# A second weight combination with shared products, copied by ScalarE into the accumulator's bank

## The chip, the cores and the metric

The kernel runs on one core of a Trainium2 chip. The metric is device time in microseconds (us). Engines are named as in the profile: PE is TensorE (PEld its weight loads), DVE VectorE, ACT ScalarE, POOL GpSimd, SP SyncE.

## The reference

A residual block of four modulated 1-D convolutions over x of 128 samples x 64 channels x 1024 positions, in float32. Each sample has its own weights: the layer's shared weights, scaled by the sample's style and normalised.

```python
def _layer(x, style, w, b, mw, mb, typ):
    s = style @ mw.T + mb
    weight = SCALE * w * s[:, None, :, None]
    demod = lax.rsqrt(jnp.sum(weight * weight, axis=(2, 3)) + EPS)
    weight = weight * demod[:, :, None, None]
    if typ == 'same':
        out = vmap(conv_same)(x, weight) + b
    elif typ == 'upsample':
        out = blur(vmap(conv_up)(x, weight) + b, 2.0 * blur_k, (1, 1))
    elif typ == 'downsample':
        out = vmap(conv_down)(blur(x, blur_k, (2, 2)), weight) + b
    return out

out = x
for i, typ in enumerate(('same', 'upsample', 'same', 'downsample')):
    out = _layer(out, style, weights[i], biases[i], mod_w[i], mod_b[i], typ)
return x + out
```

## The kernel before, in words

Since no layer has a nonlinearity, the kernel folds the four convolutions of a sample into one filter of nine taps of 64 x 64 weights, and then convolves x with it. The samples go in 32 **quads** of four. Four samples fill the array: each product is four matmuls of 64 x 64, one for each quarter of the array (the loops over rows and cols in HALF), and in the profile each matmul is two MATMUL records with a weight load each.

For a quad the filter is made in four steps. **scale3** (ACT) scales layer 3's weights into two wd tiles. **stage1** combines them with layer 2's weights in PSUM (psS), and ACT and DVE scale the result into an S tile. From iteration 0 on it is split: stage1_a has three products, after which ACT copies blocks 0 to 3 of S; stage1_b has two products, after which DVE makes blocks 4 and 5 (two scalar_tensor_tensor), and POOL adds block 0 onto block 2. A block is 64 columns. **stage2** (R) convolves S with the table E, which holds the nine taps of layer 1 with the blur in it; it has nine products, of three blocks where the tap's number is even and of two where it is odd, 23 blocks in all, into psR; ACT scales psR into two R tiles. **stage3** (W) combines R with layer 0's weights in two parts, and ACT scales them into Wf, from which DVE makes the tiles H (combine_a, combine_b).

The convolution itself takes five products of three taps each (conv0 to conv4, all through product()), 340 columns wide, on x as it is (T04, T3) or combined by DVE and POOL (in_g01, in_g2, in1, in2, in3, in04). conv0 to conv3 accumulate in psA of the quad, conv4 in Y; DVE combines them (sum1, sum2), and ACT makes the outputs (output), which SP stores.

The order on every engine is written out by hand in the loop over q. Iteration q finishes quad q, while it convolves n = q + 1, makes the filter of c = q + 2 (stage2, stage3), and S of s = q + 3. For most q, PE's order is: stage2(c), conv4(q), stage3(c, 0), conv3(n), stage3(c, 1), conv0(q, 0), conv1(n, 0), stage1_a(s), conv1(n, 1, 2), conv0(q, 1), stage1_b(s), conv0(q, 2), conv2(n). ACT's order at the end of an iteration is: S of stage1_a, output(q, 1), output(q, 0), scale3(s + 1), then R of the next iteration. DVE's is: sum1(n), the two S instructions, and then sum2 at the start of the next iteration.

The iterations in SLOTS (1 to 3, 5 to 7, 9, 12, 14, 19, 25) have other products in the place of stage1_a; stage1_a then stands in the place of stage1_b, and stage1_b behind conv2's first tap. EXTRA hangs small work on certain places.

PSUM has eight banks, and psS, psR, psW and psE all take turns in one pair of them (the pool ps_w has one buffer for each of the tags u0 and u1). psA has two buffers of two banks each, of which 340 of 512 columns are used; Y has the last pair. A matmul with start=True marks the whole bank as empty; one with start=False adds where a matmul has written since, and overwrites elsewhere.

Of the kernel before, what the change touches and what calls it, by code (L numbers as in the profile page):

```python
# [48 lines left out]
F32 = mybir.dt.float32  # L49
AF = mybir.ActivationFunctionType  # L50
ALU = mybir.AluOpType
# [3 lines left out]
C = 64  # L55
# [8 lines left out]
def kernel(  # L64
# [293 lines left out]
    def scaled_copy(eng, dst, src, f):  # L358
        if eng is nc_a:
            nc_a.activation(dst, src, AF.Copy, scale=f)  # L360
        else:
            eng.tensor_scalar(dst, src, f, None, op0=ALU.mult)
# [33 lines left out]
                )  # L396

    def s_tiles(q):
        t = s_pool.tile([P, 2, 6, C], F32, tag="S", name=f"S{q}")
        return [t[:, r] for r in range(2)], t  # L400

    def flat(t):
        return t.rearrange("c a o -> c (a o)")
# [3 lines left out]
    def stage1(q, pool=None, engs=(nc_a, nc_a), between=None):  # L407

        wd = chain[q]
        ps = unit(pool or ps_w, f"psS{q}")  # L410
        for k, (at, at1) in enumerate(((0, 3), (3, 1), (1, 4))):
            tap_matmul(ps, wd, at, 2, woi[2][:, k, :], EVEN, first=k == 0)
            tap_matmul(ps, wd, at1, 1, woi[2][:, k, :], slice(1, 2), last=k == K - 1)
        if between:
            between()
        st, _ = s_tiles(q)
        for r in range(2):
            scaled_copy(engs[r], flat(st[r][:, 1:]), ps[r][:, : 5 * C], tB[:, q, r : r + 1])
        chain[q] = st
        return ps  # L420

    def stage1_a(q):

        ps = unit(ps_w, f"psS{q}")
        wd = chain[q]
        tap_matmul(ps, wd, 1, 2, w2n[:, 0, :], EVEN, first=True)
        tap_matmul(ps, wd, 2, 2, w2n[:, 2, :], EVEN)
        tap_matmul(ps, wd, 0, 1, w2n[:, 1, :], slice(1, 2))
        st, t = s_tiles(q)
        for r in range(2):  # L430
            scaled_copy(nc_a, flat(st[r][:, :4]), ps[r][:, : 4 * C], tBn[:, q, r : r + 1])
        chain[q] = wd, ps, st, t

    def stage1_b(q):

        wd, ps, st, t = chain[q]
        tap_matmul(ps, wd, 1, 1, w2n[:, 3, :], slice(3, 4))
        tap_matmul(ps, wd, 3, 1, w2n[:, 4, :], slice(4, 5), last=True)
        for r in range(2):
            p1 = st[r][:, 0:1, :].to_broadcast([P, 2, C])  # L440
            sums = ps[r][:, C : 5 * C].rearrange("c (a b o) -> c a b o", a=2, b=2)[:, :, 0]
            nc_v.scalar_tensor_tensor(
                st[r][:, 4:, :], sums, tB[:, q, r : r + 1], p1, op0=ALU.mult, op1=ALU.subtract
            )
        nc_g.tensor_add(t[:, :, 2], t[:, :, 2], t[:, :, 0])  # L445
        chain[q] = st

    def stage2(q, pool=None, engs=(nc_a, nc_a), between=None):
        st = chain[q]
        ps = unit(pool or ps_w, f"psR{q}")  # L450
        for n, e in enumerate((-2, -1, 0, 1, 2, 3, 4, 5, 6)):
            if e % 2 == 0:
                a, lo, m = slice(1, 4), e // 2 + 1, 3
            else:
                a, lo, m = slice(4, 6), (e + 3) // 2, 2
            for r, rows in enumerate(HALF):
                for c, cols in enumerate(HALF):
                    src = st[c if r == 0 else 1 - c]
                    nc.tensor.matmul(  # L459
                        ps[r][cols, lo * C : (lo + m) * C],  # L460
                        E[rows, e + 2, :],
                        src[rows, a, :],
                        start=(n == 0),
                        stop=(n == 8),
                        skip_group_check=True,
                    )
        if between:
            between()
        rt = []
        for r in range(2):  # L470
            t = r_pool.tile([P, 7, C], F32, tag="R", name=f"R{q}_{r}")
            scaled_copy(
                engs[r], t.rearrange("c t o -> c (t o)"), ps[r][:, : 7 * C], tC[:, q, r : r + 1]
            )
            rt.append(t)
        chain[q] = rt
        return ps
# [191 lines left out]
    def conv0(q, *groups):  # L669
        product(q, 0, banks(q), groups)  # L670
# [401 lines left out]
    def layers(i, j):  # L1072
# [15 lines left out]
        (7, 0): lambda: const_rest(1, REST, after(0)),  # L1088
        (7, 1): lambda: const_rest(2, REST, after(0)),
        (7, 2): lambda: (table_b(REST), zeros()),  # L1090
        (8, 0): lambda: (setup_x(0), setup_x(1)),
        (9, 0): lambda: (setup0(), setup3()),
        (10, 0): lambda: rest0(0),
        (10, 1): lambda: setup1(0),
# [15 lines left out]
    def extra(*at):  # L1110
        EXTRA.get(at, lambda: None)()

    for q in range(NQ):
        n, c, s = q + 1, q + 2, q + 3
        if q == 1:
            nc.sync.dma_start(Xe, x_ends)
        if n == NQ:
            for i, queue in enumerate((nc.sync, nc_a)):
                output(q, 1, i, nc_v)
                store(q, i, slice(1, 2), queue)  # L1120
            conv4(q)
            for i, (eng, queue) in enumerate(zip(BOTH, (nc.sync, nc_a))):
                output(q, 2, i, eng)
                store(q, i, slice(2, K), queue)
            conv0(q, *range(K))
            for i, (eng, queue) in enumerate(zip(BOTH, (nc_a, nc.sync))):
                output(q, 0, i, eng)
                store(q, i, slice(0, 1), queue)
            break
        if c < NQ:  # L1130
            stage2(c)
        if n < NQ - 1:
            sum2(q)
        if n < NQ - 1:
            if q == 0:
                in_g01(n)
            if q == 1:
                in_g2(n)
                load(n + NX)
            combine_a(n)  # L1140
            combine_b(n)
            if q == 0:
                in_g2(n)
                load(n + NX)

        if n == NQ - 1:

            conv3(n, ps_w)
            copy_m3(n)
            conv4(q, 0, 1)  # L1150
            for i in range(2):
                output(q, 1, i)
            conv1(n)
            sum1(n)
            conv4(q, 2)
            for i in range(2):
                output(q, 2, i)
                store(q, i, slice(1, K))
            in04(n, PAIR[0])
            in04(n, PAIR[1])  # L1160
            conv0(q, 0)
            conv2(n)
            conv0(q, 1, 2)
            sum2(n)
            for i in range(2):
                output(q, 0, i)
                store(q, i, slice(0, 1))
            continue

        conv4(q)  # L1170
        if q == 0:
            var_matmul(PART[1], var_of(PART[1]), start=False)
            var_root(PART[1], var_of(PART[1]))
            var_newton(PART[1])
            table_A(PART[1], dm[:, 2, PART[1]])
            for of in (table_C, vector_c0, table_3, vector_Da):
                of(PART[1])
        if q < 2:
            in1(n, nc_v)
            in2(n, nc_v)  # L1180
        for i in range(2):
            output(q, 2, i)
        if c < NQ:
            stage3(c, 0)
        conv3(n)
        copy_m3(n)
        extra(q, 0)
        in04(n)
        if q:
            in3(c)  # L1190
        if q > 1:
            in_g01(c)
        if c < NQ:
            stage3(c, 1)
        conv0(q, 0)
        conv1(n, 0)
        if q in SLOTS:
            slot(*SLOTS[q])
        elif s < NQ:
            stage1_a(s)  # L1200
        conv1(n, 1, 2)
        for i in range(2):
            output(q, 1, i)
        if q > 1:
            in_g2(c)
            load(c + NX)
        extra(q, 1)
        if n == NQ - 2:
            combine_a(n + 1, lambda: sum1(n))
            combine_b(n + 1)  # L1210
        else:
            sum1(n)
        if q == 0:
            in3(c)
        if q == 1:
            in_g01(c)
        conv0(q, 1)
        if q in SLOTS:
            stage1_a(s)
        elif s < NQ:  # L1220
            stage1_b(s)
        conv0(q, 2)
        for i in range(2):
            output(q, 0, i)
        conv2(n, 0)
        if q in SLOTS:
            stage1_b(s)
        if q == 0:
            in_g01(c)
        if q == 1:  # L1230
            in_g2(c)
            load(c + NX)
        if q and c < NQ - 1:
            in1(c, nc_g)
            in2(c, nc_g)
        extra(q, 2)
        if s + 1 < NQ:
            scale3(s + 1)
        conv2(n, 1, 2)
        if n == NQ - 2:  # L1240
            sum2(n)
            in1(n + 1, nc_v)
            in2(n + 1, nc_v)
        for i in range(2):
            store(q, i)
# [78 lines left out]
```

## Time and profile before

| | |
|---|---|
| median of 3 runs | 484.76 us (483.73 to 484.83) |
| the profiled execution | 483.65 us |
| its span | 481.9 us |
| PE, busy | 475.3 us, 99% |
| PE weight loads, busy | 374.3 us, 78% |
| DVE, busy | 385.0 us, 80% |
| ACT, busy | 289.9 us, 60% |
| POOL, busy | 133.9 us, 28% |
| granted clock | 0.999 |

Busy time is the share of the span in which the engine has at least one instruction running; the records of PE overlap each other. "Idle before" is the time that an engine waited in front of an instruction, with what ended it behind the arrow. In the chain of waits each piece starts where the one before it ends.

### The profile page before, as it was taken

How to read it: one execution, taken by the hardware profiler on the slowest of the kernel's cores; microseconds unless marked ns; L12 is line 12 of the kernel's file. 1: busy time of each engine (PE TensorE's matmuls, PEld its weight loads, DVE VectorE, ACT ScalarE, POOL GpSimd, SP SyncE). 2: the span in 40 equal slices, each digit the busy share in tenths (PEclk: the TensorE clock that was granted, in tenths of full speed). 3: DMA queues.
4: the chain of work that ended last, by engine and by line, in shares of the span. 5: the costliest groups of instructions: out<-in, count | busy, mean ns of one | idle time of the engine just before them, and what ended most of it. 6: DMA issues, size and time to landing. Idle time of an engine off the chain costs nothing.

```text
span 481.9 us, 22176 instructions
## 1 busy us (share of the span) xinstructions
PE 475.3 (99%) x10048; PEld 374.3 (78%) x10048; DVE 385.0 (80%) x632; ACT 289.9 (60%) x580; POOL 133.9 (28%) x169
## 2 busy tenths in 40 slices
PE   8999999999999999999999999999999999999995
PEld 7977778777777777778888788878888878888863
DVE  4899989887789868878857898758988876888784
ACT  5465676665675556656656665656566656566542
POOL 2533124534415233303333212333113332213300
PEclk9999999999999999999999999999999999999999
DMA  7116364454422454342553434542344443245225
GB/s 238 58 62 207 110 213 136 177 178 178 158 98 102 176 178 174 102 150 109 177 177 86 145 128 177 177 175 75 129 157 177 178 176 130 85 163 176 91 88 175
DMA packets 20527, 70.42 MB, mean 146 GB/s; under 512 B 2320, under 2 KB 4048, under 8 KB 20432
## 3 DMA queue, kind: packets, MB, share of 16 engines
q1 hardware_dynamic: 19840, 68.30, 40.4%
q8 instruction: 79, 1.29, 1.1%
q10 hardware_dynamic: 592, 0.69, 0.5%
q14 instruction: 16, 0.13, 0.1%
HBM read 35.36 MB, written 33.62 MB: 143 GB/s over the span
## 4 chain that ended last, share of the span: by engine, by line
PE 97%; DVE 1%; issue 0%; ACT 0%; ACTq 0%; DVEq 0%
PE psA L613 45%; PE psR L459 17%; PE psW L500 15%; PE Y L613 11%; PE psS L389 5%; PE psE L844 2%; PE Y L336 1%; PE Y L181 1%; PE psM L205 0%; DVE T L600 0%; DVE o L684 0%; ACT o L682 0%; DVE y L664 0%; DVE y L521 0%; ACTq L687 0%
## 5 line engine op out<-in xcount | busy, mean ns | idle before, releaser
L613 PE MATMUL psA<-T,H 64*64 64x340 f32 x2304 | 193.8, 446 | 0.2 <-DVE y L521 0.2
L613 PEld LDWEIGHTS psA<-T,H 64*64 64x64 f32 x2304 | 99.8, 133 | 46.3 <-issue 11.9
L445 POOL TENSOR_TENSOR S<-S 128x128 f32<-128x128 f32 x29 | 13.9, 478 | 291.2 <-ACT S L360 291.2
L459 PE MATMUL psR<-S,E 64*64 64x192 f32 (+1 forms) x2304 | 87.0, 299 | 0.0
L459 PEld LDWEIGHTS psR<-S,E 64*64 64x64 f32 x2304 | 81.4, 133 | 6.0
L360 ACT ACTIVATE R<-psR,tC 128x448 f32<-128x448 f32 x63 | 36.6, 630 | 68.7 <-PE psR L459 67.2
L521 DVE SCALAR_TENSOR_TENSOR G<-X 128x684 f32<-128x684 f32 (+1 forms) x65 | 76.1, 1206 | 0.0
L613 PE MATMUL psA<-T,Wf 64*64 64x340 f32 x768 | 75.4, 447 | 0.0
L500 PE MATMUL psW<-R,w0s 64*64 64x128 f32 (+1 forms) x1536 | 62.4, 287 | 0.0
L613 PE MATMUL Y<-T,Wf 64*64 64x340 f32 x768 | 62.0, 446 | 0.1
L360 ACT ACTIVATE Wf<-psW,t 128x384 f32<-128x384 f32 (+1 forms) x126 | 56.3, 497 | 9.2 <-PE psW L500 8.5
L500 PEld LDWEIGHTS psW<-R,w0s 64*64 64x64 f32 x1536 | 52.6, 133 | 5.8
L521 DVE SCALAR_TENSOR_TENSOR Y<-m,psA 128x680 f32<-128x680 f32 (+1 forms) x33 | 28.0, 849 | 33.4 <-PE psA L613 32.9
L600 DVE TENSOR_TENSOR T<-G 128x1368 f32<-128x1368 f32 (+1 forms) x33 | 50.7, 1539 | 0.1
L521 DVE SCALAR_TENSOR_TENSOR y<-psA,m 128x680 f32<-128x680 f32 (+1 forms) x33 | 27.8, 844 | 28.3 <-PE psA L613 27.6
L682 ACT ACTIVATE o<-Y,tb,td 128x340 f32<-128x340 f32 x63 | 36.6, 630 | 22.0 <-ACT R L360 17.4
L389 PEld LDWEIGHTS psS<-wd,w2n 64*64 64x64 f32 x1160 | 40.0, 133 | 9.5 <-ACT S L360 0.2
L586 POOL TENSOR_TENSOR T<-G 128x684 f32<-128x684 f32 x28 | 46.5, 1660 | 1.4 <-DVE G L521 1.4
L591 POOL TENSOR_TENSOR T<-G 128x684 f32<-128x684 f32 x28 | 46.5, 1659 | 0.0
L682 ACT ACTIVATE o<-psA,tb,td 128x340 f32<-128x340 f32 x63 | 36.6, 633 | 15.3 <-PE psA L613 15.3
L613 PEld LDWEIGHTS Y<-T,Wf 64*64 64x64 f32 x768 | 35.1, 133 | 13.5 <-issue 0.6
L521 DVE SCALAR_TENSOR_TENSOR H<-Wf 128x384 f32<-128x384 f32 x64 | 39.4, 616 | 0.0
(146 smaller groups left out, 530.9 us busy)
## 6 DMA issues: line engine op xcount, KB each, us to landing
X<-in_x SPq DMA_DIRECT2D x64, 516.0 KB, 4.6
out<-o SPq DMA_DIRECT2D x60, 510.0 KB, 5.3
out<-o SPq DMA_DIRECT2D x5, 170.0 KB, 3.4
out<-o SPq DMA_DIRECT2D x2, 340.0 KB, 3.0
Xe<-in_x_ends SPq DMA_DIRECT2D x1, 512.0 KB, 6.8
out<-o ACTq DMA_DIRECT2D x3, 170.0 KB, 3.5
par<-in_params SPq DMA_DIRECT2D x2, 192.0 KB, 3.3
par<-in_params SPq DMA_DIRECT2D x2, 96.0 KB, 2.6
```

Source lines behind the costliest of these rows:

```text
L360: nc_a.activation(dst, src, AF.Copy, scale=f)
L389: nc.tensor.matmul(ps[r][cols, at * C : (at + n) * C], weight[rows], wd[c if r == 0 else 1 - c][rows, taps], start=first, stop=last, skip_ ...
L445: nc_g.tensor_add(t[:, :, 2], t[:, :, 2], t[:, :, 0])
L459: nc.tensor.matmul(ps[r][cols, lo * C : (lo + m) * C], E[rows, e + 2, :], src[rows, a, :], start=(n == 0), stop=(n == 8), skip_group_check ...
L500: nc.tensor.matmul(ps[r][cols, at : at + m * C], w0s[kind][rows, k, :], rt[c][rows, first : first + K * (m - 1) + 1 : K, :], start=(n == 1 ...
L521: nc_v.scalar_tensor_tensor(out, x, f, y, op0=ALU.mult, op1=op)
L586: eng.tensor_add(t[:, :, 0, :NJ], plane(g, 2), plane(g, 1))
L591: eng.tensor_sub(t[:, :, 1, :NJ], plane(g, 2), plane(g, 1))
L600: nc_v.tensor_sub(t[:, pairs, :, :NJ], both(a, PL), both(b, 1))
L613: nc.tensor.matmul(ps[s][cols, :NB], w, Ts[q, tag][rows, c, i, g : g + NB], start=(g == 0 and m == 3), stop=(g == K - 1), skip_group_check ...
L682: nc_a.activation(dst, src, AF.Identity, bias=add, scale=d3)
L844: nc.tensor.matmul(ps[r][cols, : HB * n].rearrange("c (b j) -> c b j", j=n), weight(i, r, c)[rows], moving(i, r, c)[rows], start=(i == 0), ...
```

## The change

In the quads concerned, stage2 takes 20 blocks of columns in place of 23, in 17 products in place of nine. Two sums that several blocks of R have in common are made once: share(c + 1) puts three products of one block each into the free columns 344 to 471 of psA of quad q, between stage1_b and conv0's last tap. share_copy(c + 1) then has ACT copy these two blocks, each twice, into blocks 1 to 4 of the bank pair where R is going to be accumulated. In the next iteration stage2_rest adds the other 14 products onto that, with start=False throughout: three are two blocks wide, the others one.

This takes, beside S, two sums of its blocks (share_sums, one DVE addition, for which the S tile grows from six blocks to eight) and six differences of taps (Ed, three POOL subtractions in iteration 8). S of a quad has to be there before share() of the iteration ahead, so from iteration 8 on s is q + 4; iteration 8 makes S of two quads, the first with the unsplit stage1, and iteration 7 scales layer 3's weights of two quads. The products of stage1_a and stage1_b move up by one block in their bank, so that blocks 1 to 4 are the ones which matmuls have written there.

By the order of the built program the first of the two copies waits for the last matmul of conv0(q) and for DVE's first S instruction of that iteration (they still read the bank pair), the second for DVE's second S instruction; stage2_rest waits for the two copies.

```diff
@@ -396,7 +396,7 @@
                 )
 
     def s_tiles(q):
-        t = s_pool.tile([P, 2, 6, C], F32, tag="S", name=f"S{q}")
+        t = s_pool.tile([P, 2, 8, C], F32, tag="S", name=f"S{q}")
         return [t[:, r] for r in range(2)], t
 
     def flat(t):
@@ -415,7 +415,7 @@
             between()
         st, _ = s_tiles(q)
         for r in range(2):
-            scaled_copy(engs[r], flat(st[r][:, 1:]), ps[r][:, : 5 * C], tB[:, q, r : r + 1])
+            scaled_copy(engs[r], flat(st[r][:, 1:6]), ps[r][:, : 5 * C], tB[:, q, r : r + 1])
         chain[q] = st
         return ps
 
@@ -423,32 +423,105 @@
 
         ps = unit(ps_w, f"psS{q}")
         wd = chain[q]
-        tap_matmul(ps, wd, 1, 2, w2n[:, 0, :], EVEN, first=True)
-        tap_matmul(ps, wd, 2, 2, w2n[:, 2, :], EVEN)
-        tap_matmul(ps, wd, 0, 1, w2n[:, 1, :], slice(1, 2))
+        tap_matmul(ps, wd, 2, 2, w2n[:, 0, :], EVEN, first=True)
+        tap_matmul(ps, wd, 3, 2, w2n[:, 2, :], EVEN)
+        tap_matmul(ps, wd, 1, 1, w2n[:, 1, :], slice(1, 2))
         st, t = s_tiles(q)
         for r in range(2):
-            scaled_copy(nc_a, flat(st[r][:, :4]), ps[r][:, : 4 * C], tBn[:, q, r : r + 1])
+            scaled_copy(nc_a, flat(st[r][:, :4]), ps[r][:, C : 5 * C], tBn[:, q, r : r + 1])
         chain[q] = wd, ps, st, t
 
     def stage1_b(q):
 
         wd, ps, st, t = chain[q]
-        tap_matmul(ps, wd, 1, 1, w2n[:, 3, :], slice(3, 4))
-        tap_matmul(ps, wd, 3, 1, w2n[:, 4, :], slice(4, 5), last=True)
+        tap_matmul(ps, wd, 2, 1, w2n[:, 3, :], slice(3, 4))
+        tap_matmul(ps, wd, 4, 1, w2n[:, 4, :], slice(4, 5), last=True)
         for r in range(2):
             p1 = st[r][:, 0:1, :].to_broadcast([P, 2, C])
-            sums = ps[r][:, C : 5 * C].rearrange("c (a b o) -> c a b o", a=2, b=2)[:, :, 0]
+            sums = ps[r][:, 2 * C : 6 * C].rearrange("c (a b o) -> c a b o", a=2, b=2)[:, :, 0]
             nc_v.scalar_tensor_tensor(
-                st[r][:, 4:, :], sums, tB[:, q, r : r + 1], p1, op0=ALU.mult, op1=ALU.subtract
+                st[r][:, 4:6, :], sums, tB[:, q, r : r + 1], p1, op0=ALU.mult, op1=ALU.subtract
             )
         nc_g.tensor_add(t[:, :, 2], t[:, :, 2], t[:, :, 0])
         chain[q] = st
+        whole[q] = t
+
+    whole, shared_ps = {}, {}
+    Ed = const.tile([P, 6, C], F32, name="Ed")
+
+    def tap_differences():
+
+        d = Ed[:, :4].rearrange("c (a b) o -> c a b o", a=2)
+        for b in range(2):
+            nc_g.tensor_sub(d[:, :, b], E[:, 4 * b : 4 * b + 5 : 4], E[:, 2:7:4])
+        nc_g.tensor_sub(Ed[:, 4:], E[:, 3:8:4], E[:, 5:6].to_broadcast([P, 2, C]))
+
+    def share_sums(q):
+        t = whole[q]
+        nc_v.tensor_add(t[:, :, 6:8], t[:, :, 1:5:3], t[:, :, 2:6:3])
+
+    def chain_matmul(dst, weight, st, slots, last=False):
+        for r, rows in enumerate(HALF):
+            for c, cols in enumerate(HALF):
+                nc.tensor.matmul(
+                    dst[r][cols],
+                    weight[rows],
+                    st[c if r == 0 else 1 - c][rows, slots, :],
+                    start=False,
+                    stop=last,
+                    skip_group_check=True,
+                )
+
+    def share(q, ps):
+
+        at = [NB + 4 + i * C for i in range(3)]
+        p12, p34 = ([b[:, i:j] for b in ps] for i, j in zip(at, at[1:]))
+        chain_matmul(p12, E[:, 2], chain[q], slice(6, 7))
+        chain_matmul(p34, E[:, 6], chain[q], slice(6, 7))
+        chain_matmul(p34, E[:, 5], chain[q], slice(7, 8), True)
+        shared_ps[q] = [b[:, at[0] : at[2]] for b in ps]
+
+    def share_copy(q):
+
+        ps = unit(ps_w, f"psR{q}")
+        for r in range(2):
+            src = shared_ps[q][r].rearrange("c (a o) -> c a o", a=2)
+            nc_a.copy(
+                ps[r][:, C : 5 * C].rearrange("c (a b o) -> c a b o", a=2, b=2),
+                src[:, :, None, :].to_broadcast([P, 2, 2, C]),
+            )
+        shared_ps[q] = ps
+
+    def stage2_rest(q):
+
+        ps = shared_ps.pop(q)
+        block = lambda i, n=1: [b[:, i * C : (i + n) * C] for b in ps]
+        apart = [b[:, : 4 * C].rearrange("c (a b o) -> c a b o", a=2, b=2)[:, :, 0] for b in ps]
+        plan = (
+            (apart, E[:, 0], slice(1, 4, 2)),
+            (block(1), Ed[:, 0], slice(2, 3)),
+            (block(2), Ed[:, 1], slice(1, 2)),
+            (block(3), E[:, 2], slice(3, 4)),
+            (block(3), Ed[:, 2], slice(2, 3)),
+            (block(4), Ed[:, 3], slice(1, 2)),
+            (block(4), E[:, 4], slice(3, 4)),
+            (block(5, 2), E[:, 8], slice(2, 4)),
+            (block(5), E[:, 6], slice(3, 4)),
+            (block(1, 2), E[:, 1], slice(4, 6)),
+            (block(2), E[:, 3], slice(4, 5)),
+            (block(3), Ed[:, 4], slice(5, 6)),
+            (block(4), Ed[:, 5], slice(4, 5)),
+            (block(5), E[:, 7], slice(5, 6)),
+        )
+        for n, (dst, weight, slots) in enumerate(plan):
+            chain_matmul(dst, weight, chain[q], slots, n == len(plan) - 1)
+        return ps
 
     def stage2(q, pool=None, engs=(nc_a, nc_a), between=None):
         st = chain[q]
-        ps = unit(pool or ps_w, f"psR{q}")
-        for n, e in enumerate((-2, -1, 0, 1, 2, 3, 4, 5, 6)):
+        shared = q in shared_ps
+        ps = stage2_rest(q) if shared else unit(pool or ps_w, f"psR{q}")
+        for n, e in enumerate(() if shared else (-2, -1, 0, 1, 2, 3, 4, 5, 6)):
             if e % 2 == 0:
                 a, lo, m = slice(1, 4), e // 2 + 1, 3
             else:
@@ -1088,7 +1161,7 @@
         (7, 0): lambda: const_rest(1, REST, after(0)),
         (7, 1): lambda: const_rest(2, REST, after(0)),
         (7, 2): lambda: (table_b(REST), zeros()),
-        (8, 0): lambda: (setup_x(0), setup_x(1)),
+        (8, 0): lambda: (setup_x(0), setup_x(1), tap_differences()),
         (9, 0): lambda: (setup0(), setup3()),
         (10, 0): lambda: rest0(0),
         (10, 1): lambda: setup1(0),
@@ -1110,8 +1183,14 @@
     def extra(*at):
         EXTRA.get(at, lambda: None)()
 
+    AHEAD = 8
+
+    def sharing(q):
+        return q > AHEAD and q not in SLOTS and q + 4 < NQ
+
     for q in range(NQ):
-        n, c, s = q + 1, q + 2, q + 3
+        n, c, s = q + 1, q + 2, q + 3 + (q >= AHEAD)
+        slot_here = q in SLOTS or q == AHEAD
         if q == 1:
             nc.sync.dma_start(Xe, x_ends)
         if n == NQ:
@@ -1196,6 +1275,8 @@
         conv1(n, 0)
         if q in SLOTS:
             slot(*SLOTS[q])
+        elif q == AHEAD:
+            stage1(s - 1)
         elif s < NQ:
             stage1_a(s)
         conv1(n, 1, 2)
@@ -1215,16 +1296,24 @@
         if q == 1:
             in_g01(c)
         conv0(q, 1)
-        if q in SLOTS:
+        if slot_here:
             stage1_a(s)
         elif s < NQ:
             stage1_b(s)
+        if sharing(q + 1) and not slot_here:
+            share_sums(s)
+        if sharing(q):
+            share(c + 1, banks(q))
         conv0(q, 2)
+        if sharing(q):
+            share_copy(c + 1)
         for i in range(2):
             output(q, 0, i)
         conv2(n, 0)
-        if q in SLOTS:
+        if slot_here:
             stage1_b(s)
+            if sharing(q + 1):
+                share_sums(s)
         if q == 0:
             in_g01(c)
         if q == 1:
@@ -1236,6 +1325,8 @@
         extra(q, 2)
         if s + 1 < NQ:
             scale3(s + 1)
+        if q == AHEAD - 1:
+            scale3(s + 2)
         conv2(n, 1, 2)
         if n == NQ - 2:
             sum2(n)
```

The prediction calls products of one block (64 columns) narrow.

## The prediction

> **What bounds the kernel now.** I read the page first, then the chain of waits.
>
> ```profile
> span 481.9 us, 22176 instructions
> ...
> PE 475.3 (99%) x10048; PEld 374.3 (78%) x10048; DVE 385.0 (80%) x632; ACT 289.9 (60%) x580; POOL 133.9 (28%) x169
> ...
> PE 97%; DVE 1%; issue 0%; ACT 0%; ACTq 0%; DVEq 0%
> PE psA L613 45%; PE psR L459 17%; PE psW L500 15%; PE Y L613 11%; PE psS L389 5%; PE psE L844 2%; PE Y L336 1%; PE Y L181 1%; PE psM L205 0%; DVE T L600 0%; DVE o L684 0%; ACT o L682 0%; DVE y L664 0%; DVE y L521 0%; ACTq L687 0%
> ```
>
> The chain that ends last is PE for 97%, and hardly anything else releases it: PE runs back to back, so the time is the sum of what its matmuls take from each other's start. The stage that changes is psR at L459, 17%. Busy time overlaps, so what a product costs has to come from the pieces of the chain, which follow each other without overlap (start, length, what, records):
>
> ```profile
> 200.97 0.23 PE psS L389 x16
> 201.20 2.29 PE psA L613 x32
> 203.49 2.50 PE psR L459 x72
> 205.99 1.72 PE Y L613 x24
> 207.70 1.52 PE psW L500 x48
> ...
> 210.94 0.76 PE psW L500 x24
> ...
> 216.18 0.55 PE psS L389 x24
> ```
>
> and from the shapes behind psR:
>
> ```profile
> L459 PE MATMUL psR<-S,E 64*64 64x192 f32 x1280 | 85.5, 323 | 0.0
> ...
> L459 PE MATMUL psR<-S,E 64*64 64x128 f32 x1024 | 55.8, 269 | 0.0
> ```
>
> A product is four matmuls of 64x64, one for each quarter of the array, and each is two records, so eight records. The two narrow products of stage1_b (x16, 64 columns each) take 0.23: a 64-column product costs g64 = 0.115 us; I use 0.116. Stage1_a is two products of 128 and one of 64: (0.55 - 0.115) / 2 gives g128 = 0.2175. psR is 1280/256 = 5 products of 192 and 1024/256 = 4 of 128 in each of 32 quads: (2.50 - 4 x 0.2175) / 5 gives g192 = 0.326. As a check, stage3 part 1 is one of 192 and two of 128, which makes 0.761 where the chain has 0.76; part 0 is twice that, and it has 1.52.
>
> **The change on PE.** By the order of the built program the new form is used for 14 quads, not 15: R 13, 14, 16, 18 to 21, 23 to 27, 29 and 30. The others lie before iteration 9, in iterations with a slot, or at the end. Each of the 14 loses 9 products (2.50 us) and gets 17: 3 narrow ones in share(), then in stage2_rest 3 of 128 columns and 11 of 64. That is 3 x 0.2175 + 14 x 0.116 = 2.28 us, 0.22 less; times 14, **3.1 us less**. Columns fall from 23 to 20 blocks, 13%, but time by 9%, since the narrow product has a larger fixed part.
>
> Making S one iteration sooner needs one extra stage1 in iteration 8. It is the unsplit form, with three products of 128 and three of 64 (1.00 us) where stage1_a and stage1_b together take 2 x 0.2175 + 3 x 0.116 = 0.78: **0.22 more, once**. At the end one iteration loses its stage1, so the count of quads is the same. Net: 2.9 us less.
>
> g64 from both sides: continuing the step from 192 to 128 columns gives 0.109 (gain 4.3 in all). Upwards, the nearest row is a longer run with narrow products in it, at the start of the kernel:
>
> ```profile
> 14.09 1.16 PE psS L389 x48
> ```
>
> That is three products of 128 and three of 64, whose sum by my prices is 1.00; put wholly on the narrow ones it makes g64 = (1.16 - 0.65) / 3 = 0.17 (a loss of 7.7 in all). But the run starts behind other work and wider products did not pay, so I stay by the row from mid-kernel. One product writes two blocks that are not neighbours, which no row shows: from 0.2175 (as one of 128) to 0.232 (as two narrow ones), 0 to 0.2 us in all; I take 0, since reading such blocks costs stage1_a nothing.
>
> **The change on ACT.** share_copy puts two copies of 256 columns, PSUM to PSUM, on ACT for each of the 14 quads. The queue around that place, in an iteration that will share:
>
> ```profile
> 265.70 1.16 ACT L360 ACTIVATE R<-psR,tC 128x448 f32<-128x448 f32 x2 [2.12 <-PE psR L459]
> ...
> 273.17 0.84 ACT L360 ACTIVATE S<-psS,tBn 128x256 f32<-128x256 f32 x2 [1.02 <-PE psS L389]
> ...
> 274.09 0.46 POOL L445 TENSOR_TENSOR S<-S 128x128 f32<-128x128 f32 x1 [10.51 <-ACT S L360]
> ...
> 274.37 0.86 DVE L521 SCALAR_TENSOR_TENSOR y<-psA,m 128x680 f32<-128x680 f32 x1 [0.46 <-PE psA L613]
> ...
> 275.15 0.60 DVE L442 SCALAR_TENSOR_TENSOR S<-psS,tB,S 128x128 f32<-128x128 f32 x2
> ...
> 275.40 1.94 PE L613 MATMUL psA<-T,H 64*64 64x340 f32 x24
> 275.67 1.16 ACT L682 ACTIVATE o<-psA,tb,td 128x340 f32<-128x340 f32 x2 [0.55 <-PE psA L613]
> ...
> 276.73 1.01 ACT L360 ACTIVATE wd<-w3x,tA 128x320 f32<-128x320 f32 x2
> ...
> 277.39 0.87 DVE L521 SCALAR_TENSOR_TENSOR Y<-m,psA 128x680 f32<-128x680 f32 x1 [1.64 <-PE psA L613]
> ```
>
> ```profile
> L703 ACT COPY raw<-psE 128x256 f32<-128x256 f32 x2 | 0.6, 375 | 1.8 <-PE psE L844 1.8
> ```
>
> The nearest row for one copy is 375 ns; the scaled pair of S took 0.84 in all. I take 0.75 for a pair, between 0.65 (overlapped like the S pair) and 0.84. The first copy waits for the end of conv0(q,2), because it reads that bank, and both wait for DVE's two S instructions, which still read the bank that the copy writes. Behind them stand output(q,0) and the next scale3, and then R, for which PE would wait. In the rows' times: conv0(q,2) ends at 275.40 + 3 x 0.116 = 275.75, ACT sees it 0.27 later (275.67 against 275.40 in the rows), DVE is done at 275.75, so the copies run from 276.02 to 276.77, the outputs to 277.9, scale3 to 278.9. PE does conv2 in 1.72 (to 277.47), and then needs the copies: 0.7 us to spare. stage2_rest ends 1.93 later, at 279.40, and R can start 0.27 after that; ACT is free 0.8 before. So the 2.12 us of idle in front of R hides it all: cost 0. Were this cover gone, the price is what R is late, and then stage3 part 0, PE's next reader of R, waits behind conv4.
>
> Iteration 7 gets two more scale3 instructions (1.0 us) and iteration 8 a pair of S copies; both stand ahead of an R with idle of the same kind, cost 0.
>
> **The change on DVE and POOL.** share_sums is one DVE addition of 256 columns, 0.44 us by the nearest row; the second fence is the group of y in the stretch from 199 to 202 us alone:
>
> ```profile
> L884 DVE TENSOR_TENSOR Ue<-raw,a 128x256 f32<-128x256 f32 x2 | 0.8, 441 | 0.0
> ```
>
> ```profile
> L521 DVE SCALAR_TENSOR_TENSOR y<-psA,m 128x680 f32<-128x680 f32 x1 | 0.9, 865 | 0.1
> ```
>
> It stands behind the S instructions and ahead of sum2's Y, which has 1.64 us of idle in front: hidden. In iterations with a slot S comes later and the same idle is 0.53 us (the next fence), still more than 0.44.
>
> ```profile
> 322.45 0.87 DVE L521 SCALAR_TENSOR_TENSOR Y<-m,psA 128x680 f32<-128x680 f32 x1 [0.53 <-PE psA L613]
> ```
>
> What is late next is sum1. The stretch from sum2 to sum1 loses 2.50 - 1.93 = 0.57 us of PE time and no DVE work, so DVE's 0.46 of idle in front of y (row 274.37) is used up and y is 0.1 late. The worst is iteration 11 with an idle of 0.1 (the second fence): 0.47 late. conv2 waits for y: it ends at 274.37 + 0.86 = 275.23, conv2 starts at 275.40 before and at 275.75 after, so 0.5 us is there. Cost 0, in iteration 11 up to 0.1, once. The POOL addition that share_sums needs (274.09, 0.46 long) is over before S starts at 275.15. POOL's three new instructions for Ed fall into iteration 8, where it idles 5.75 us before its S addition, cost 0:
>
> ```profile
> 155.56 0.46 POOL L445 TENSOR_TENSOR S<-S 128x128 f32<-128x128 f32 x1 [5.75 <-ACT S L360]
> ```
>
> No DMA is added. The stores wait for outputs that come some 0.75 us later after the shift of ACT's queue; nothing follows from it before the same output tile is used two iterations on.
>
> **The sum.** The profiled execution took 483.65 us (span 481.9): 483.65 - 3.1 + 0.2 = 480.75. The median of the three runs shown is 484.76, 1.1 above it, and the same 2.9 leads to **481.9 us**.
>
> **The rivals.**
>
> *Issue (slower).* PE may not be able to issue narrow products at 0.116 for long: in mid-kernel they come two at a time between products of 340 columns, so a queue can have filled before. Now 14 products, 11 of them narrow, stand in one run. The row of 48 records gives 1.16 / 48 = 24 ns a record; were that a floor on a record in a run, g64 would be 8 x 0.024 = 0.193 and the stage 0.65 + 14 x 0.193 = 3.36, 0.86 more than now: +12.0 + 0.2, some **497 us**. It decides against the change from g64 = (2.50 - 0.65 - 0.2 / 14) / 14 = 0.131, or 16 ns a record. For it: no long narrow run is in the trace. Against it: 16 records in 0.23 are 14 ns each, and the two prices between which a step shows (g192 and g128) fall nearly with the columns, in runs of 72 records. [...]
>
> A milder floor, g64 from 0.123 to 0.138, eats most of the gain: each 0.001 is 0.2 us, so 0.13 means about **484.6 us**.
>
> *ACT hands over too late.* If a pair of copies takes 1.5 us or more instead of 0.75 (both wait on two engines, and no row shows a copy into PSUM), R is late, and PE waits in front of stage3 in 14 iterations. The cover is the 0.8 above, and 0.3 more, since PE does conv4 (1.72) before stage3 while R needs 0.27 + 1.16; and the copies themselves have 0.7 before PE wants them. 0.2 beyond the cover costs 14 x 0.2 = 2.8: **484.7 us**, no change. Against it: that takes copies of twice the row.
>
> *DVE.* If y's lateness reaches PE, 0.1 in five iterations and 0.5 in one: 1.0 us, **482.9 us**.
>
> *It doesn't do what it says.* Column blocks fall as said; what it doesn't do is 15 quads, which is in the sum.
>
> **How the numbers follow.** Forecast 0.70, DVE 0.05, ACT 0.10, mild floor 0.05, full floor 0.10. A measurement can tell about 0.3% (1.45 us) from no change. The forecast and DVE lie below that: faster 0.75. ACT and the mild floor are within: 0.15. The full floor is slower: 0.10. The likeliest case alone runs from 480.5 (g64 of 0.109) to 482.9. The range leaves out the full floor and half of ACT and the mild floor above, and goes to 480.2 below, since the runs of one kernel lie 1.1 us apart: 480.2 to 484.3.
>
> **What would show it.** The chain's pieces of psR: 1.93 us for the 14 products of a quad, and 0.35 more ahead of conv0's last tap. Narrow records that start 58 ns apart in each quarter bear g64 out; 65 or more refute it. ACT's idle in front of R should fall from 2.12 to about 0.7 and stay above 0; DVE's in front of y to 0. PE's matmuls of psR, psW or psA with waits on ACT or DVE, at 14 places, would make the prediction wrong.

## The result and the profile after

The changed kernel takes 492.31 us (median of 6 executions, 488.6 to 492.66) against 484.42 for the kernel before (6 executions, 483.73 to 484.83): a ratio of 1.015, with a 95% interval of 1.012 to 1.0181 (the ratios compare the means of the executions, here 491.6 and 484.4). By the medians it is 7.9 us slower, where 2.9 less was forecast, and the time lies outside the range. The profiled execution took 488.6 us, the fastest of the six.

The page of the changed kernel (the same rows as before; the row of queue 8 gives packets, MB and share):

```profile
span 486.7 us, 24044 instructions
...
PE 474.8 (98%) x10952; PEld 387.6 (80%) x10952; DVE 395.9 (81%) x644; ACT 298.0 (61%) x608; POOL 140.3 (29%) x171
...
q8 instruction: 86, 1.41, 1.2%
...
PE 97%; issue 1%; DVE 1%; ACT 0%; ACTq 0%; DVEq 0%
PE psA L686 45%; PE psW L573 15%; PE Y L686 11%; PE psR L532 9%; PE psR L466 6%; PE psS L389 5%; PE psE L917 2%; PE psA L466 1%; PE Y L181 1%; PE Y L336 0%; PE psM L205 0%; DVE y L594 0%; ACT o L755 0%; PE psM L232 0%; DVE o L757 0%
```

and the same row of queue 8 on the page of the kernel before:

```profile
q8 instruction: 79, 1.29, 1.1%
```

PE's busy time fell by half a microsecond while the span grew by 4.8, so PE stands still more. "Issue", idle time for which the profile shows no cause, was 0% of the chain and is 1%. PE's waits in the changed kernel (total us, times, longest) say where:

```profile
PE psR L466 <- issue: 3.6, 6, 1.3
PE psA L686 <- DVE y L594: 1.6, 2, 1.4
```

Two new things, then: PE stops in the middle of the run of narrow products with nothing to wait for that the profile shows, and once conv2 waits for y. First the chain of waits (start, length, what, records) at an undisturbed quad and at two with a stop:

```profile
191.62 1.94 PE psR L466 x112
...
279.74 1.61 PE psR L466 x82
281.35 1.35 issue
282.70 0.50 PE psR L466 x17
...
368.85 1.70 PE psR L466 x85
370.56 1.00 issue
371.56 0.46 PE psR L466 x16
```

The first has the 1.93 us that the prediction gave the 14 products. In the others a stop of a microsecond or more lies in the run, and the work around it is 1.61 + 0.50 = 2.11 and 1.70 + 0.46 = 2.16 us (the chain passes over some of the 112 records). The idle time counts from the modelled end of the last matmul, whose end otherwise overlaps the next one, so a stop costs some 0.2 more than the idle: these two runs take 3.46 and 3.16 us in place of 1.94. Added up from the first start to the last, the 14 runs take 33.1 us here and 27.7 in the last version below, where none stops: the stops cost 5.4 us in this execution, not 3.6.

**What the stops have in common.** The page has 2 x 10952 = 21904 instructions of PE (matmuls and weight loads) and 86 packets of instructions, 255 a packet, and 1.41 MB / 86 = 16.4 KB; before it is 20096 / 79 = 254. So PE's code comes in blocks of some 255 of these instructions, half of them matmuls. The view by stretches counts the matmuls up to a moment; here are three stretches that end where PE goes on after a stop (and, second, one that ends at 277.12):

```profile
0.00:266.94 266.94, 263.12 (x5959) 1.00 0.43 149
0.00:277.12 277.12, 273.29 (x6211) 1.00 0.42 145
0.00:282.69 282.69, 277.52 (x6342) 1.00 0.43 150
0.00:356.15 356.15, 350.60 (x8129) 1.00 0.42 148
```

From one stop to the next it is 6342 - 5959 = 383 and 8129 - 6342 = 1787 matmuls: 3 times 127.67 and 14 times 127.64, half of 255 again, to within 0.2. Seven of the 14 runs have a stop (the seventh, 0.26 us, is too short for the list of waits), and all seven lie whole multiples of 127.65 matmuls apart, to within a tenth of a matmul. PE stops where one block ends and the next has not come. The boundary before the stop that ends at 282.70 was passed at about 277.1 (131 matmuls earlier), and the queues show what happened between, first from 277.2 to 280.2, then to 281.3:

```profile
q1 hardware_dynamic: 270, 1.02, 93.1%
```

```profile
q1 hardware_dynamic: 110, 0.42, 97.0%
q8 instruction: 1, 0.02, 5.1%
```

For some 3 us the loads of X and the stores kept the 16 DMA engines at 93% and no block was fetched; its packet started at 280.34, and PE went on 2.36 us later. In all seven stops PE goes on 2.26 to 2.42 us after its packet starts. What differs is how long the packet waits. With the boundaries placed by that period of 127.65, the packets between 185 and 455 us start 0.3 us behind the boundary (median of 21) where data take under 10% of the DMA engines in the microsecond behind it, and 1.6 us, at most 3.2 (also 21), where they take over 90%. Both transfers are issued ahead of or into the run (SP's timeline):

```profile
275.95 0.81 SPq L146 DMA_DIRECT2D X<-in_x  x2
...
279.27 0.87 SPq L760 DMA_DIRECT2D out<-o  x2
```

In the kernel before a block lasts 481.9 / 79 = 6.1 us on the mean, which gives a late fetch that time; now 14 products x 16 = 224 instructions are used up in 1.94 us.

**The wait for y**, in iteration 10, and two rows of ACT (timeline):

```profile
186.41 2.34 DVE L893 SCALAR_TENSOR_TENSOR g<-par,g 128x192 f32<-128x192 f32 x2
...
186.77 1.76 POOL L659 TENSOR_TENSOR T<-G 128x684 f32<-128x684 f32 x1
...
188.68 0.85 DVE L594 SCALAR_TENSOR_TENSOR y<-psA,m 128x680 f32<-128x680 f32 x1
...
189.68 1.09 PE L686 MATMUL psA<-T,H 64*64 64x340 f32 x12 [1.44 <-DVE y L594]
...
193.64 1.16 ACT L360 ACTIVATE R<-psR,tC 128x448 f32<-128x448 f32 x2 [1.16 <-PE psR L466]
...
263.54 0.63 ACT L489 COPY psR<-psA 128x256 f32<-128x256 f32 x2 [0.94 <-PE psA L686]
```

The kernel before, same place:

```profile
185.60 0.88 DVE L820 SCALAR_TENSOR_TENSOR g<-par,g 128x192 f32<-128x192 f32 x2
...
186.22 1.78 POOL L586 TENSOR_TENSOR T<-G 128x684 f32<-128x684 f32 x1
```

The two g instructions of setup1(0) took 0.88 us and were done before POOL's addition had been running for 0.3; now DVE comes to them 0.8 later, the second one runs beside POOL's 1.76 and takes 1.70 itself, and y, next on DVE, is late for conv2. ACT is as forecast: a pair of copies in 0.63 us, and 1.16 of idle left in front of R (after the 2.12 of before) in an undisturbed quad.

### The profile page after: what moved, and what is told of

Same layout as the page of the kernel before. It is cut to its first block, busy times and chain, and to the rows that moved or that the text cites. A ratio compares the mean times of both kernels' runs of the same rounds, so it can differ in the third digit from the quotient of the medians.

```text
span 486.7 us, 24044 instructions
## 1 busy us (share of the span) xinstructions
PE 474.8 (98%) x10952; PEld 387.6 (80%) x10952; DVE 395.9 (81%) x644; ACT 298.0 (61%) x608; POOL 140.3 (29%) x171
## 3 DMA queue, kind: packets, MB, share of 16 engines
q8 instruction: 86, 1.41, 1.2%
## 4 chain that ended last, share of the span: by engine, by line
PE 97%; issue 1%; DVE 1%; ACT 0%; ACTq 0%; DVEq 0%
PE psA L686 45%; PE psW L573 15%; PE Y L686 11%; PE psR L532 9%; PE psR L466 6%; PE psS L389 5%; PE psE L917 2%; PE psA L466 1%; PE Y L181 1%; PE Y L336 0%; PE psM L205 0%; DVE y L594 0%; ACT o L755 0%; PE psM L232 0%; DVE o L757 0%
## 5 line engine op out<-in xcount | busy, mean ns | idle before, releaser
L686 PE MATMUL psA<-T,H 64*64 64x340 f32 x2304 | 198.2, 446 | 1.6 <-DVE y L594 1.6
L686 PEld LDWEIGHTS psA<-T,H 64*64 64x64 f32 x2304 | 109.8, 133 | 39.6 <-issue 6.7
L686 PE MATMUL psA<-T,Wf 64*64 64x340 f32 x768 | 78.4, 447 | 0.0
L573 PE MATMUL psW<-R,w0s 64*64 64x128 f32 (+1 forms) x1536 | 65.2, 287 | 0.0
L686 PE MATMUL Y<-T,Wf 64*64 64x340 f32 x768 | 63.0, 446 | 0.1
L573 PEld LDWEIGHTS psW<-R,w0s 64*64 64x64 f32 x1536 | 55.1, 133 | 5.1 <-issue 0.3
L659 POOL TENSOR_TENSOR T<-G 128x684 f32<-128x684 f32 x28 | 46.7, 1669 | 10.9 <-DVE G L594 10.9
L664 POOL TENSOR_TENSOR T<-G 128x684 f32<-128x684 f32 x28 | 49.1, 1753 | 0.0
L532 PE MATMUL psR<-S,E 64*64 64x192 f32 (+1 forms) x1296 | 48.9, 299 | 0.0
L532 PEld LDWEIGHTS psR<-S,E 64*64 64x64 f32 x1296 | 45.5, 133 | 3.5
L594 DVE SCALAR_TENSOR_TENSOR y<-psA,m 128x680 f32<-128x680 f32 (+1 forms) x33 | 27.7, 843 | 25.1 <-PE psA L686 24.3
L686 PEld LDWEIGHTS psA<-T,Wf 64*64 64x64 f32 x768 | 35.6, 133 | 6.1
```

Source lines behind the costliest of these rows:

```text
L532: nc.tensor.matmul(ps[r][cols, lo * C : (lo + m) * C], E[rows, e + 2, :], src[rows, a, :], start=(n == 0), stop=(n == 8), skip_group_check ...
L573: nc.tensor.matmul(ps[r][cols, at : at + m * C], w0s[kind][rows, k, :], rt[c][rows, first : first + K * (m - 1) + 1 : K, :], start=(n == 1 ...
L594: nc_v.scalar_tensor_tensor(out, x, f, y, op0=ALU.mult, op1=op)
L659: eng.tensor_add(t[:, :, 0, :NJ], plane(g, 2), plane(g, 1))
L664: eng.tensor_sub(t[:, :, 1, :NJ], plane(g, 2), plane(g, 1))
L686: nc.tensor.matmul(ps[s][cols, :NB], w, Ts[q, tag][rows, c, i, g : g + NB], start=(g == 0 and m == 3), stop=(g == K - 1), skip_group_check ...
```

## The experiments

Theory: late **blocks** of instructions cost most of the loss, and DVE behind POOL in iteration 10 some 1.5 us. Rivals: the shift of S itself; ACT's handover; narrow products that are dear in themselves.

**S one iteration sooner, nothing else.**

```diff
     def sharing(q):
-        return q > AHEAD and q not in SLOTS and q + 4 < NQ
+        return False
```

> The changed kernel with S one iteration sooner but without any sharing: no share(), no sums, no copies, and stage2 with its nine old products. Blocks theory (in the changed kernel PE runs out of instructions in the run of narrow products, because the next block of 16384 bytes is fetched too late; plus one wait of conv2 for y in iteration 10): nothing of this is left here, so before + 0.2 us, about 484.6, no PE idle put down to issue inside psR. Rival, the shift itself costs (scale3, S and their buffers held an iteration longer): some us over before, up to the whole 7.9 of the changed kernel. Rival, narrow products cost more than their price: before + 0.2 as well.

484.4 us against 483.77 before: ratio 1.0013 (1.0001 to 1.0024). The shift costs 0.05 to 1.2 us, which holds the forecast 0.2; PE has no issue inside psR. The shift alone is not the cause.

**Sharing as it is, but the nine old products.** They overwrite the copies, so share() and the copies are extra work here.

```diff
-        shared = q in shared_ps
-        ps = stage2_rest(q) if shared else unit(pool or ps_w, f"psR{q}")
-        for n, e in enumerate(() if shared else (-2, -1, 0, 1, 2, 3, 4, 5, 6)):
+        ps = shared_ps.pop(q, None) or unit(pool or ps_w, f"psR{q}")
+        for n, e in enumerate((-2, -1, 0, 1, 2, 3, 4, 5, 6)):
```

> The changed kernel with share(), the sums on DVE and the copies on ACT as they are, but stage2 with its nine old products, which overwrite what was copied and still wait for the copies. Blocks theory: no run of narrow products, so no idle inside psR; before + 0.2 + 14 x 0.35 for share() = +5.1, and +1.5 for the wait in iteration 10, about 491. psR runs stay at 2.50 us. Rival, the handover by ACT (copies late for PE): the loss stays on top of the added products, about 8 + 3 + 5: 499 or more, with psR's first product waiting for ACT. Rival, narrow products cost more than their price: as the blocks theory, since only the three of share() are left.

489.97 us, ratio 1.0132 (1.0117 to 1.0147): 6.2 more than before, where 6.6 was the sum (0.2 + 4.9 for share() + 1.5 for the wait for y). Its chain of waits (start, length, what):

```profile
264.52 2.35 PE psA L685 x32
266.87 2.50 PE psR L531 x72
...
281.37 2.50 PE psR L531 x72
```

From psR to psR is 14.50 us, with no wait in it; before, the row of the chain has 2.50 at 263.20 and again at 277.34, 14.14 apart. The 0.36 more is share(), which was priced at 0.35. psR follows on the conv products at once although it still waits for the copies: ACT hands over in time.

**Loads and stores behind the run, issued by ACT.**

```diff
         if c < NQ:
             stage2(c)
+        if q > AHEAD:
+            for i in range(2):
+                store(q - 1, i, queue=nc_a)
+            load(c - 1 + NX, queue=nc_a)
...
-            load(c + NX)
+            if q < AHEAD:
+                load(c + NX)
...
-        for i in range(2):
-            store(q, i)
+        if q < AHEAD:
+            for i in range(2):
+                store(q, i)
```

> The changed kernel from iteration 9 on with the loads of X and the stores of the output issued from ACT behind the next iteration's R copies, so that these transfers start after the run of narrow products in place of running through it. Blocks theory: the blocks of instructions are fetched in time, the psR runs take 1.93 to 2.05 us in all 14 quads, and the time falls by 5 to 9 us to 483 to 486; what stays is the wait in iteration 10. Rival, narrow products cost more than their price or PE cannot issue them faster: no change, about 492. Rival, the handover by ACT: no change or slower, as ACT has three more DMA issues in its queue.

496.69 us, ratio 1.0268 (1.0253 to 1.0284): the time missed what was expected by 11 us, the wrong way. But issue inside psR is gone, as expected; PE's weight loads wait elsewhere (waits of PEld, then the timeline around one such place):

```profile
PEld psW L573 <- ACT Wf L360: 19.5, 40, 1.3
```

```profile
377.22 1.56 ACTq L760 DMA_DIRECT2D out<-o  x2
...
378.82 1.35 ACTq L146 DMA_DIRECT2D X<-in_x  x2
...
380.35 1.16 ACT L755 ACTIVATE o<-Y,tb,td 128x340 f32<-128x340 f32 x2 [2.08 <-PE psW L573]
...
382.03 0.20 PEld L573 LDWEIGHTS psW<-R,w0s 64*64 64x64 f32 x4 [0.59 <-ACT Wf L360]
```

A DMA issue holds ACT for about 0.7 us. Four of them put the outputs behind, then Wf, and stage3's second part waits. So the stops go when the transfers leave the run, but this way of moving them costs more than the stops did, and PE's time around the run changed as well; the late outputs below move them without that.

**setup1(0) on DVE in iteration 9 instead of 10.**

```diff
-        (10, 1): lambda: setup1(0),
+        (9, 1): lambda: setup1(0),
```

> The changed kernel with the DVE work of setup1(0) moved from iteration 10 to iteration 9. Theory of the wait in iteration 10 (setup1's two instructions on DVE took 2.34 us in place of 0.88 beside POOL's additions and made y late for conv2): 1.4 us less than the changed kernel, about 491, the 1.44 us of idle of conv2 <- DVE y are gone. Rival, DVE is late there in any case through the sums: the wait stays and the time too, 492.3.

487.64 us, ratio 1.0082 (1.0056 to 1.0109; executions from 485.95 to 491.56). conv2's waits for y fell from 1.6 to 0.2 in its profile, as expected. By the ratios that is 2.5 to 3.3 us under the changed kernel (its second and its first measurement), where 1.4 was expected. The wait accounts for 1.4; the rest lies inside the spread of executions that still have stops (psR's issue is 2.7 us in this profile) and stays open.

**The changed kernel again**, measured beside the next three.

> The changed kernel as it is, for a second profile and beside the next three. Blocks theory: the time moves from execution to execution with the moment at which each block's fetch starts, between about 488.6 and 492.7; if the profiled one is one of the slower ones, it has more or longer idle put down to issue inside the runs of psR than the 3.6 us (6 times) of the first profile, again at block boundaries, and the wait of conv2 for y of 1.4 us is there again. Rival, a fixed cost of narrow products: the same length of every run in both profiles, and a spread as small as that of the kernel before (1.1 us).

489.94 us (488.63 to 493.18), ratio 1.0134 (1.0104 to 1.0164). The profiled execution was again the fastest, 488.63. PE's waits, then the worst quad in the chain:

```profile
PE psR L466 <- issue: 3.5, 2, 2.0
```

```profile
368.85 1.71 PE psR L466 x85
370.56 1.99 issue
372.55 0.46 PE psR L466 x16
```

The stop comes after the same 85 records as in the first profile, at the same boundary, but lasts 1.99 in place of 1.00; at the boundary of the stop of 281.35 this profile has 0.2. The packet of the block started at 369.18 in the first profile and at 370.16 in this one, 0.98 later, and PE goes on 0.99 later. The place is fixed by the program, the length by the moment at which the fetch gets through. That the executions of 491 to 493 us have more of it stays open, as none of them was profiled.

**The same shift of transfers without an issue on ACT.** ACT writes half of output plane 0 behind R, and SP's queue holds the stores and loads behind that half.

```diff
         if c < NQ:
             stage2(c)
+        if sharing(q - 1):
+            output(q - 1, 0, 1)
+            for i in (1, 0):
+                store(q - 1, i)
+            load(c - 1 + NX)
...
-            load(c + NX)
+            if not sharing(q):
+                load(c + NX)
...
-        for i in range(2):
+        for i in range(1 if sharing(q) else 2):
             output(q, 0, i)
...
-        for i in range(2):
+        for i in range(0 if sharing(q) else 2):
             store(q, i)
```

> The changed kernel, in the 13 or 14 iterations whose next one has the run of narrow products: ACT writes the second half of output plane 0 behind the R copies in place of ahead of them, and SP's queue has the two stores and then the loads of X behind it, so that they start after the run, with no DMA issue on ACT. Blocks theory: no idle put down to issue inside psR, all runs 1.93 to 2.05 us, the time is that of before + 0.2 - 3.1 + 1.5 (the wait in iteration 10 stays) = 1.4 under before, about 482.5. Rival, ACT's order now makes the outputs of Y and the Wf copies late as in the run before with issues on ACT (PE waits 0.1 to 0.6 for Wf in every such iteration): 484 to 490. Rival, narrow products are dear in themselves: no change, 488 to 492.

484.57 us, ratio 1.0025 (1.0005 to 1.0045): 5.4 less than the changed kernel beside it, though 2 over the expected time. One of the ten executions took 489.13, and no profile shows why. PE's waits have no issue in psR, and a second wait for y, which is 1.5 that the expectation didn't have:

```profile
PE psA L686 <- DVE y L594: 3.0, 3, 1.5
```

**With setup1(0) sooner as well** (both edits above).

> The late output of plane 0, stores and loads together with setup1(0) one iteration sooner. Blocks theory and the theory of the wait in iteration 10, both: before + 0.2 - 3.1 = 2.9 under before, about 481, with neither issue inside psR nor a wait of conv2 for y over 0.3 us; that would be faster than both kernels. Rival, ACT's order: 483 to 489. Rival, narrow products are dear in themselves: as the changed kernel with setup1 sooner, 487.6.

482.92 us, ratio 0.9985 (0.997 to 0.9999), 1.9 over what was expected. The timeline of iteration 11 has 1.4 of it:

```profile
201.21 2.33 DVE L893 SCALAR_TENSOR_TENSOR g<-par,g 128x192 f32<-128x192 f32 x2
201.58 1.75 POOL L659 TENSOR_TENSOR T<-G 128x684 f32<-128x684 f32 x1
...
204.47 1.95 PE L686 MATMUL psA<-T,H 64*64 64x340 f32 x24 [1.39 <-DVE y L594]
```

The other half, setup1(1), now meets POOL's addition in the same way; in the changed kernel it did not. That the missing stops shift it there is likely but not shown.

**Only the stores late**, the loads where the changed kernel has them (setup1(0) sooner; the edit of the last but one without its two changes to load).

> As the run with both (late output of plane 0, setup1 sooner), but the loads of X stay where the changed kernel has them; only the stores start after the run of narrow products. If the stores alone keep the blocks waiting: as the run with both, about 481. If the loads, which are in flight from 3.5 us ahead of the run to 1 us into it, do as much: stalls at block boundaries stay in about half of the runs, 483 to 486.

486.46 us, ratio 1.0051 (1.0033 to 1.0068), 0.5 above what was expected if the loads count as well (1.4 of wait for y is in it, as in the run before). The stops are back in the list, four of them:

```profile
PE psR L466 <- issue: 2.6, 4, 0.8
```

**Both halves of setup1 in iteration 9**, transfers late.

```diff
-        (10, 1): lambda: setup1(0),
+        (9, 1): lambda: (setup1(0), setup1(1)),
...
-        (11, 1): lambda: setup1(1),
```

> The late output of plane 0, stores and loads, with both parts of setup1 on DVE in iteration 9 (in the run with one part moved, the other one in iteration 11 took 2.33 us in place of 0.87 beside POOL's addition and conv2 waited 1.39 for y). If that wait has the cause that is named: 1.4 us under that run, about 481.5 on the same measure, 0.5% under before, and no wait of conv2 for y over 0.3 us. Rival, DVE has no room for both in iteration 9 and y is late there: a wait of up to 0.9 us in iteration 9, about 482.4.

481.97 us (480.89 to 482.76), ratio 0.9954 (0.994 to 0.9968): faster than both kernels, by 0.3% to 0.6% against the one before. Its chain, its queues from 276 to 278, and SP's timeline:

```profile
264.17 1.88 PE psR L466 x100
...
278.11 1.88 PE psR L466 x92
```

```profile
q8 instruction: 1, 0.02, 3.3%
q1 hardware_dynamic: 3, 0.01, 1.0%
```

```profile
267.85 0.81 SPq L760 DMA_DIRECT2D out<-o  x2
268.76 1.97 SPq L146 DMA_DIRECT2D X<-in_x  x2
```

The transfers start behind the run, a packet of instructions comes while data take 1.0% of the DMA engines, and from psR to psR it is 13.94 us, 0.20 under the 14.14 of before; 0.217 was forecast for a quad.

**The kernel before with the transfers late**, the edit of the late output alone.

> The kernel before (23 products, no sharing) with only the late output of plane 0, stores and loads, in the same iterations. Blocks theory: PE takes a block of the old order in about 5 us, so no fetch was late before and moving the transfers gives nothing: 1.000 of the time before, within 0.2%. Rival, the transfers slow PE or other engines in some other way, and what the later runs gained has nothing to do with narrow products: 2 us or more under before here too.

483.98 us, ratio 0.9997 (0.9987 to 1.0007). Without narrow runs the moment of the transfers is worth nothing that shows (0.6 us at most by the interval).

## Why the prediction was wrong

- **Prices of the products: right.** 1.94 us was measured for the 112 records (1.93 forecast), 0.36 for share() (0.35), 0.20 less for an iteration with both (0.217).
- **The step that failed: "The sum".** It took PE's time to be the products' durations alone, and left out what has to arrive for them. A product is 16 instructions of PE (8 matmuls and their weight loads), so 17 instead of 9 make 128 more in each of 14 quads: 1792, which is 7.0 times 255 and so the 86 - 79 packets. The bounds for g64 were sought in the price of a record; the loss lies in the supply. In the two profiles of the changed kernel the stops cost 5.4 and 4.7 us, and the first one closes to 1 us: 483.65 - 2.9 + 5.4 + 1.4 for y is 487.6, where 488.6 was measured. Over all executions, from the ratio with setup1(0) sooner (1.0082, conv2 waits no more than 0.2 for y) to that with the transfers late as well (0.9954) it is 1.28%, **6.2 us for the late blocks**. With 1.5 for y, and less the 2.2 that the version without both gains, it makes 5.5 us over before; the changed kernel is 6.5 over by its second measurement (1.34% of 484) and 7.3 by the first. The 1 to 2 us between lie within the spread of its executions, 488.6 to 493.2, and stay open; both profiles are of executions at its lower end.
- **The Issue rival** had the right place (a long run of narrow products) and the wrong cause. Where no block is late, the same run takes 1.94 us, and its test, the distance of narrow records in a quarter, comes out at the forecast 58 ns; a stopped run loses its time in one place. The sign to look for was idle without a cause.
- **ACT: right.** 0.63 us a pair (0.75 forecast), R's idle stays over 1.0 in all 14 quads (0.7 forecast), and the run with the old products shows no wait for the copies.
- **DVE: the place and size were wrong.** "in iteration 11 up to 0.1, once" took DVE's durations as fixed. y was late in iteration 10, by 1.44 us, since two instructions that came to lie beside POOL's additions take 2.34 instead of 0.88. Moving setup1 took the wait away, in two steps.
- **14 quads, and 0.2 for the shift of S: right** within what was measured.
- **The forecast 2.9 under before** is nearly what the version without stops and waits reaches: 0.9954 of 484.3 is 2.2 less (interval 1.5 to 2.9). So the gain that was priced is there; the changed kernel hides it behind the two terms that the sum left out.

## What to carry to other kernels

Price a run of short matmuls twice: by the matmuls, and by its instructions against the time in which the next block of code can come, and look at what the DMA engines do in that stretch. Here the 112 matmuls of a run took 1.94 us, so the 127.65 of a whole block would take 2.2 (an estimate), and in the seven stops PE went on 2.26 to 2.42 after the packet's start: my estimate from these numbers is that a narrow run longer than a block would stop PE even with empty queues, which no run here tried. Where a run is faster than its code comes through full queues (here 1.94 us, against a packet that data held back for 3.2), move the transfers, not the products, and not onto an engine that has no time for the issue. When work on DVE shifts by a microsecond, look at what POOL does at the new place.

## What the runs showed of the hardware

- Code of PE came in packets of 16.4 KB, one for some 255 instructions. While data kept the 16 DMA engines at 93%, none started for 3.2 us, and in the seven stops PE went on 2.26 to 2.42 us after the late one had started. In the kernel before, the chain of waits has 0% of issue; in the changed one a stop lasts up to 1.99 us.
- Two DVE instructions took 2.34 us in place of 0.88 (the second one 1.70, beside a POOL addition of 1.76), while y, with one input in PSUM, kept its 0.85 beside POOL's next one (from 188.50 on, 1.75 us). Why the one was slowed and the other not, no run shows.
- A DMA issue from ACT held it for about 0.7 us (1.56 and 1.35 for two).
